# Routed rows of a mixture of experts: 31 blocks of 256 and 9 of 128 in place of 39 of 256, with three buffers of weights

## The chip, the cores and the metric

The kernel runs as one program on one core of a Trainium2 chip. The metric is the device time of one execution in microseconds (us). TensorE (PE in the profile; its weight loads are listed apart as PEld), VectorE (DVE), ScalarE (ACT), GpSimd (POOL) and SyncE (SP) each work through their own list of instructions in order. They wait for one another only through semaphores, and DMA transfers are issued from these lists too, here mostly from SP, ACT and POOL. The TensorE clock that the chip grants varies; the profile shows it as a share of full speed.

## The reference

Two transformer layers on x of shape (4, 1024, 256), that is 4,096 rows of D = 256, all in float32. Each layer is an attention and a feed-forward part, each on the layer-normalised x and added to it. The change is in the first layer's feed-forward, a mixture of eight routed and two shared experts (H = 512 hidden values, K = 2 experts per row):

```python
def _swiglu_stacked(x, w1, b1, w2, b2, w3, b3):
    p1 = jnp.einsum('btd,ndh->nbth', x, w1) + b1[:, None, None, :]
    p2 = jnp.einsum('btd,ndh->nbth', x, w2) + b2[:, None, None, :]
    glu = jax.nn.silu(p1) * p2
    return jnp.einsum('nbth,nhd->nbtd', glu, w3) + b3[:, None, None, :]
...
scores = jax.nn.softmax(x @ gate_w + gate_b, axis=-1)
weights, indices = jax.lax.top_k(scores, K)
routed_all = _swiglu_stacked(x, rw1, rb1, rw2, rb2, rw3, rb3)
...
routed = jnp.sum(weights[..., None] * gathered, axis=2)
shared = _swiglu_stacked(x, sw1, sb1, sw2, sb2, sw3, sb3).mean(axis=0)
return shared + routed
```

The reference computes all eight experts for all rows and picks two; a kernel has to compute only the two that were chosen, which is 8,192 rows of expert work in all. How many rows each expert gets is known only at run time.

## The kernel before

The whole kernel is one function, `two_layers`. It keeps x in SBUF as 32 tiles of 128 rows. A scheduler orders the instructions of each engine from the program's order, their dependencies and the number of buffers of each tile; nothing is ordered by hand in this part. The first feed-forward (from L508) runs in these steps.

1. The eight units of 512 rows are normalised and transposed (`xnT_f0`), and the gate's logits are computed (`gate`, L567). Meanwhile SP loads the first shared expert's weights and fills the scratch array `xs_d` in device memory with zeros (L689).
2. `shared(e, weights, u)` (L634) is the feed-forward of a shared expert on unit u: 16 up-matmuls of 512 columns (L643), an activation on ACT (L651) and a product on DVE (L652) for each of the four blocks f of 128 hidden values, then 16 down-matmuls of 256 columns (L660). The units of the first shared expert are spread over the time in which the routing is computed.
3. `choose` (L589) marks the two experts of each row on DVE. Running sums by matmul (L720, L725) give each row its place among the rows of its expert (`pos`). DVE then finds how many blocks of BT = 256 rows each expert needs (`over`, `blocks`), where each expert begins (`ends`, `begins`), the slot of each row (`slot`), the expert that owns each block (`owner`), and each block's biases (`b_blk`).
4. POOL scatters the rows to their slots in `xs_d` with 64 indirect DMAs (L799). Under them TensorE goes on with shared units.
5. The routed blocks (L817): NBLK = 39 blocks of 256 rows, enough for every split of the 8,192 rows over eight experts. For block n, SP reads the owner from SBUF into a register (L818), loads that expert's weights w1, w2 and w3, 512 KB each (`load_expert`, L625; pool `epool`, two buffers), the bias b3 spread over all partitions (L823), and the block's rows `xb` (L827, two buffers). TensorE transposes the rows (L833), ACT copies them (`xbT`, L839), and the up-matmuls take 128x128 pieces of w1 and w2 as stationary and xbT, 256 columns, as moving operand (L847). Two f share one tile of two PSUM banks. ACT and DVE make `glu_b` of it (L857, L860). The down-matmuls take glu_b as stationary and w3 as moving operand (L871), DVE adds b3 (`yb`, L879), and ACT issues the write to `ys_d` (L885).
6. The second shared expert's other six units (L890), and under them POOL gathers each row's two results from `ys_d` (L898) and DVE adds them, weighted, to x (L904).

The scheduler places the transposes of the next block between the down-matmuls of a block, where TensorE would wait for the products.

Of the kernel before, what the change touches and what calls it, by code (L numbers as in the profile page):

```python
# [8 lines left out]
F32 = mybir.dt.float32  # L9
F32R = mybir.dt.float32r  # L10
BF16 = mybir.dt.bfloat16
I32 = mybir.dt.int32
U32 = mybir.dt.uint32
AF = mybir.ActivationFunctionType
ALU = mybir.AluOpType
AX = mybir.AxisListType
PSUM = bass.MemoryType.PSUM

P = 128
D = 256  # L20
NB = 4
S = 1024
NT = NB * S // P
# [6 lines left out]
E = 8  # L30
FF = 512
NF = FF // P
# [7 lines left out]
def two_layers(  # L40
# [33 lines left out]
    nc = tc.nc  # L74
# [28 lines left out]
    for i in range(NT):  # L103
# [15 lines left out]
        out=dsel,  # L119
        in_=dsel,  # L120
# [384 lines left out]

    with ExitStack() as lc:  # L508
        wpool = lc.enter_context(tc.tile_pool(name="f0_w", bufs=1))
        epool = lc.enter_context(tc.tile_pool(name="f0_e", bufs=2))  # L510
        pool = lc.enter_context(tc.tile_pool(name="f0", bufs=2))
        xnT = wpool.tile([P, 2, NT * P], F32, name="xnT_f0")
        dram = lc.enter_context(tc.tile_pool(name="f0_d", bufs=1, space=bass.MemoryType.DRAM))
        NE = E + 2
        BT = 2 * P
        NBLK = NT * P * 2 // BT + E - 1
        NSHARE = NT * P // BT

        xs_d = dram.tile([NBLK * BT, D], F32, name="xs_d")
        ys_d = dram.tile([NBLK * BT, D], F32, name="ys_d")  # L520
        gw = wpool.tile([P, 2, E], F32, name="gw")
        nc.sync.dma_start(out=gw, in_=gate0_w.rearrange("(k p) e -> p k e", p=P))
        gb = wpool.tile([P, E], F32, name="gb")
# [21 lines left out]
        )  # L545
        ones_b = wpool.tile([P, P], BF16, name="ones_b")
        nc.gpsimd.memset(ones_b, 1.0)
        full_i = wpool.tile([P, NSHARE], I32, name="full_i")
        nc.gpsimd.iota(full_i, pattern=[[BT, NSHARE]], base=0, channel_multiplier=0)
        full = wpool.tile([P, 1, NSHARE], F32, name="full")  # L550
        nc.vector.tensor_copy(full[:, 0, :], full_i)
        blk_i = wpool.tile([P, NBLK], I32, name="blk_i")
        nc.gpsimd.iota(blk_i, pattern=[[1, NBLK]], base=0, channel_multiplier=0)
        blk = wpool.tile([P, NBLK, 1], F32, name="blk")
        nc.vector.tensor_copy(blk[:, :, 0], blk_i)

# [32 lines left out]
        def choose():  # L589


            def t2(name):
                return small.tile([P, NT, 1], F32, tag=f"{name}_g", name=name)

            def wide(a):
                return a.to_broadcast([P, NT, E])

            v = nc.vector
            m = t2("m")
            v.tensor_reduce(m[:, :, 0], logits, AX.X, ALU.max)  # L600
            v.tensor_tensor(logits, logits, wide(m), ALU.subtract)
            pr = wpool.tile([P, NT, E], F32, name="pr")
            nc.scalar.activation(pr, logits, AF.Exp)
            sm = t2("sm")
            v.tensor_reduce(sm[:, :, 0], pr, AX.X, ALU.add)
            v.reciprocal(sm, sm)
            v.tensor_tensor(pr, pr, wide(sm), ALU.mult)

            for k in range(2):
                v.tensor_reduce(weight[k][:, :, 0], pr, AX.X, ALU.max)  # L610
                eq = wpool.tile([P, NT, E], F32, name=f"eq{k}")
                v.tensor_tensor(eq, pr, wide(weight[k]), ALU.is_equal)
                v.tensor_tensor(eq, eq, down.to_broadcast([P, NT, E]), ALU.mult)
                ck = t2("ck")
                v.tensor_reduce(ck[:, :, 0], eq, AX.X, ALU.max)
                v.tensor_tensor(picked[k], eq, wide(ck), ALU.is_equal)
                if k == 0:
                    v.scalar_tensor_tensor(pr, picked[0], -2.0, pr, ALU.mult, ALU.add)
            v.tensor_tensor(marks, picked[0], picked[1], ALU.add)
# [64 lines left out]
        first = load_expert(sw1[0], sw2[0], sw3[0])  # L684
        zeros = wpool.tile([P, 1, D], F32, name="zeros")
        nc.gpsimd.memset(zeros, 0.0)
        xs_fill = xs_d[:, :].rearrange("(p n r) d -> n p r d", p=P, r=13)
        for n in range(NBLK * 2 // 13):
            nc.sync.dma_start(out=xs_fill[n], in_=zeros.to_broadcast([P, 13, D]))  # L689


        roots(0, NT)
# [31 lines left out]
        for i in range(NT):  # L724
# [9 lines left out]
        nc.vector.tensor_copy(pos, pos_ps)  # L734

        v = nc.vector
        over = wpool.tile([P, E, NSHARE], F32, name="over")
        v.tensor_tensor(
            over,
            pos[:, NT, :].unsqueeze(2).to_broadcast([P, E, NSHARE]),  # L740
            full.to_broadcast([P, E, NSHARE]),
            ALU.is_gt,
        )
        blocks = wpool.tile([P, E], F32, name="blocks")
        v.tensor_reduce(blocks, over, AX.X, ALU.add)
        ends = blocks
        for step in (1, 2, 4):
            sums = wpool.tile([P, E], F32, name=f"ends{step}")
            v.tensor_copy(sums[:, :step], ends[:, :step])
            v.tensor_tensor(sums[:, step:], ends[:, step:], ends[:, :-step], ALU.add)  # L750
            ends = sums
        begins = wpool.tile([P, 1, E], F32, name="begins")
        v.tensor_tensor(begins[:, 0, :], ends, blocks, ALU.subtract)
        v.tensor_scalar(begins, begins, float(BT), None, ALU.mult)
        v.tensor_tensor(
            pos[:, :NT, :], pos[:, :NT, :], begins.to_broadcast([P, NT, E]), ALU.add
        )
        slots = []
        for k in range(2):
            v.tensor_tensor(picked[k], picked[k], pos[:, :NT, :], ALU.mult)  # L760
# [3 lines left out]
            v.tensor_copy(slot, slot_f)  # L764
            slots.append(slot)

        past = wpool.tile([P, NBLK, E], F32, name="past")
        v.tensor_tensor(
            past,
            ends.unsqueeze(1).to_broadcast([P, NBLK, E]),  # L770
            blk.to_broadcast([P, NBLK, E]),
            ALU.is_le,
        )
        owner = wpool.tile([P, NBLK, 1], F32, name="owner")
        v.tensor_reduce(owner[:, :, 0], past, AX.X, ALU.add)
        v.tensor_scalar(owner, owner, E - 1.0, None, ALU.min)
        owner_i = wpool.tile([P, NBLK], I32, name="owner_i")
        v.tensor_copy(owner_i, owner[:, :, 0])
        v.tensor_tensor(
# [34 lines left out]
            shared(E + 1, second, u)  # L814


        for n in range(NBLK):  # L817
            e = nc.sync.value_load(owner_i[0:1, n : n + 1], min_val=0, max_val=E - 1)  # L818
            w1_t, w2_t, w3_t = load_expert(
                *(w[bass.ds(e, 1)].rearrange("e k f -> (e k) f") for w in (rw1, rw2, rw3))  # L820
# [4 lines left out]
            )  # L825
            xb = pool.tile([P, 2, D], F32, tag="xb", name="xb", bufs=2)
            nc.sync.dma_start(  # L827
                out=xb, in_=xs_d[n * BT : (n + 1) * BT, :].rearrange("(a p) d -> p a d", p=P)
            )
            ps = one_bank()  # L830
            for kc in range(2):
                for a in range(2):
                    nc.tensor.transpose(  # L833
                        ps[:, (2 * kc + a) * P : (2 * kc + a + 1) * P],
                        xb[:, a, kc * P : (kc + 1) * P],
                        ident,
                    )
            xbT = pool.tile([P, 2, BT], F32, tag="xbT", name="xbT")
            nc.scalar.copy(xbT.rearrange("p k t -> p (k t)"), ps)  # L839
            glu = pool.tile([P, NF, BT], F32, tag="glu", name="glu_b")  # L840
            for fp in range(NF // 2):
                ps = two_banks()
                for m, w_t in enumerate((w1_t, w2_t)):
                    for ff in range(2):
                        f = 2 * fp + ff
                        for kc in range(2):
                            mm(  # L847
                                ps[:, (2 * m + ff) * BT : (2 * m + ff + 1) * BT],
                                lhsT=w_t[:, kc, f * P : (f + 1) * P],
                                rhs=xbT[:, kc, :],  # L850
                                start=(kc == 0),
                                stop=(kc == 1),
                            )
                for ff in range(2):
                    f = 2 * fp + ff
                    act = pool.tile([P, BT], F32, tag="act", name="act_b", bufs=3)
                    nc.scalar.activation(  # L857
                        act, ps[:, ff * BT : (ff + 1) * BT], AF.Silu, bias=b_blk[0][:, f, n : n + 1]
                    )
                    nc.vector.scalar_tensor_tensor(  # L860
                        glu[:, f, :],
                        ps[:, (2 + ff) * BT : (3 + ff) * BT],
                        b_blk[1][:, f, n : n + 1],
                        act,
                        ALU.add,
                        ALU.mult,
                    )
            ps = one_bank()
            for a in range(2):
                for f in range(NF):  # L870
                    mm(  # L871
                        ps[:, a * D : (a + 1) * D],
                        lhsT=glu[:, f, a * P : (a + 1) * P],
                        rhs=w3_t[:, f, :],
                        start=(f == 0),
                        stop=(f == NF - 1),
                    )
            yb = pool.tile([P, 2, D], F32, tag="yb", name="yb")
            nc.vector.tensor_tensor(  # L879
                yb,  # L880
                ps.rearrange("p (a d) -> p a d", a=2),
                b3_t.to_broadcast([P, 2, D]),
                ALU.add,
            )
            nc.scalar.dma_start(  # L885
                out=ys_d[n * BT : (n + 1) * BT, :].rearrange("(a p) d -> p a d", p=P), in_=yb
            )


# [848 lines left out]
```

## Time and profile before

| | |
|---|---|
| median of 3 runs | 2569.44 us (2560.59 to 2582.25) |
| the profiled execution | 2580.51 us, span 2578.6 us |
| mean granted TensorE clock | 0.941 |
| busy over the span | PE 2328.3 us (90%), PEld 1389.6 (54%), DVE 1396.7 (54%), ACT 986.0 (38%), POOL 640.4 (25%) |
| up-matmuls of the routed blocks, L847 | 1,248 records, 275.8 us busy, from 729.0 us on |
| down-matmuls, L871 | 624 records, 161.8 us busy |
| transposes, L833 | 156 records, 29.6 us busy |
| weights of routed experts | 117 transfers of 512 KB |

How to read it: times are counted from the first instruction. One f32 matmul of the program appears as two records on PE, each with a weight load on PEld, so 16 up-matmuls are 32 records. A record's own duration contains the latency through the array, and successive records overlap; how fast they follow each other is read from their starts. In rows of the timeline the columns are start, duration, engine, line, operation, tiles and count, and in brackets the engine's idle time before the row and what ended it.

### The profile page before, as it was taken

The numbers are of one execution on the slowest core, as the hardware profiler recorded it, in microseconds if no ns is written. First come the engines' busy times: TensorE is split into PE (matmuls) and PEld (weight loads), VectorE is DVE, ScalarE is ACT, GpSimd is POOL, SyncE is SP. The second block draws the span as 40 slices with busy tenths as digits, with TensorE's granted clock in tenths as the row PEclk, the third lists the DMA queues.
The fourth block names the chain that finished last, engine by engine and source line by source line (L and its number), as shares of the span: only waits on it lengthen the run. The fifth ranks groups of instructions, "written<-read, shape, count | busy, mean of one in ns | idle before, by whom it ended". The sixth has DMA issues, their size and how long they took to land.

```text
span 2578.6 us, 42321 instructions
## 1 busy us (share of the span) xinstructions
PE 2328.3 (90%) x16882; PEld 1389.6 (54%) x16882; DVE 1396.7 (54%) x2272; ACT 986.0 (38%) x1345; POOL 640.4 (25%) x741
## 2 busy tenths in 40 slices
PE   6999999899999999999957999999999999997534
PEld 3566666566578888885533444444444444443322
DVE  6445445514222222224536777676767798994293
ACT  1333333221122222221112666565656565665311
POOL 2333333601700000004340013122221211124354
PEclk8998999899999999999976999999999999998667
DMA  3000000510266666663143231312131312100134
GB/s 92 17 10 10 10 13 8 166 48 23 104 185 196 194 192 194 194 192 88 51 98 68 52 74 52 67 43 68 43 68 43 67 43 67 43 19 11 54 118 131
DMA packets 202976, 207.52 MB, mean 80 GB/s; under 512 B 89128, under 2 KB 163496, under 8 KB 202780
## 3 DMA queue, kind: packets, MB, share of 16 engines
q1 hardware_dynamic: 179292, 163.37, 23.4%
q0 software_dynamic: 11792, 30.18, 3.9%
q10 hardware_dynamic: 11696, 11.27, 1.3%
q8 instruction: 133, 2.18, 0.4%
q14 instruction: 63, 0.52, 0.1%
HBM read 141.49 MB, written 58.80 MB: 78 GB/s over the span
## 4 chain that ended last, share of the span: by engine, by line
PE 72%; DVE 15%; ACT 4%; issue 4%; DMA 2%; POOL 2%; SPq 0%; POOLq 0%; ACTq 0%; DVEq 0%
PE two L847 10%; PE two L1416 10%; PE acc L1431 8%; PE two L643 7%; DVE tops L1381 6%; PE two L329 5%; PE two L1374 4%; PE acc L871 4%; PE two L258 2%; PE two L1296 2%; PE misc L660 2%; PE acc L660 2%; PE two L321 2%; PE acc L396 1%; DVE glu_b L860 1%
## 5 line engine op out<-in xcount | busy, mean ns | idle before, releaser
L1381 DVE TENSOR_REDUCE tops<-two 128x2 f32<-128x1024 f32 x512 | 619.0, 1217 | 126.7 <-PE two L1374 124.7
L1424 ACT ACTIVATE pT<-two 128x1024 f32<-128x1024 f32 x512 | 523.5, 1025 | 329.1 <-PE two L1416 324.5
L1431 PE MATMUL acc<-pT,v_t 128*32 128x256 f32 x4096 | 345.0, 397 | 5.4 <-ACT pT L1424 5.4
L1416 PE MATMUL two<-q_st,k_st 64*128 64x512 f32 x1024 | 261.2, 503 | 32.2 <-DVE tops L1381 19.7
L847 PE MATMUL two<-xbT,w_t 128*128 128x256 f32 x1248 | 275.8, 379 | 0.7 <-ACT xbT L839 0.7
L847 PEld LDWEIGHTS two<-xbT,w_t 128*128 128x128 f32 x1248 | 237.0, 190 | 33.1 <-ACT xbT L839 0.9
L1374 PE MATMUL two<-k_st,q_st 64*128 64x512 f32 x1024 | 232.1, 421 | 20.1 <-DMA k_st<-halves 9.3
L643 PE MATMUL two<-xnT_f,w_t 128*128 128x512 f32 x512 | 229.8, 601 | 3.1 <-DVE glu L652 3.1
L1416 PEld LDWEIGHTS two<-q_st,k_st 64*128 64x128 f32 x1024 | 97.2, 185 | 225.0 <-issue 127.9
L860 DVE SCALAR_TENSOR_TENSOR glu_b<-two,b_blk,act_b 128x256 f32<-128x256 f32 x156 | 75.3, 483 | 249.4 <-ACT act_b L857 249.4
L1416 PE MATMUL two<-top_st,minus 64*128 64x512 f32 x1024 | 208.2, 401 | 0.0
L857 ACT ACTIVATE act_b<-two,b_blk 128x256 f32<-128x256 f32 x156 | 74.0, 474 | 330.6 <-PE two L847 287.6
L898 POOL DMA_INDIRECT yr<-ys_d,slot x64 | 61.4, 960 | 538.1 <-DMA ys_d<-yb 471.1
L1431 PEld LDWEIGHTS acc<-pT,v_t 128*32 128x32 f32 x4096 | 86.8, 108 | 167.9 <-issue 145.8
L871 PE MATMUL acc<-w_t,glu_b 128*128 128x256 f32 x624 | 161.8, 392 | 6.4
L1374 PEld LDWEIGHTS two<-k_st,q_st 64*128 64x128 f32 x1024 | 107.6, 191 | 92.4 <-DVE tops L1381 28.9
L643 PEld LDWEIGHTS two<-xnT_f,w_t 128*128 128x128 f32 x512 | 96.3, 192 | 111.7 <-issue 105.7
L355 DVE TENSOR_REDUCE top<-two 128x4 f32<-128x768 f32 (+1 forms) x128 | 112.5, 919 | 71.3 <-PE two L329 71.3
L381 POOL TENSOR_SCALAR_AFFINE_SELECT pT<-pT 128x1024 f32<-128x1024 f32 x64 | 70.4, 1100 | 305.5 <-ACT pT L378 305.5
L378 ACT ACTIVATE pT<-two 128x768 f32<-128x768 f32 (+1 forms) x128 | 93.7, 783 | 121.2 <-PE two L329 120.7
L651 ACT ACTIVATE act<-two,bT 128x512 f32<-128x512 f32 x64 | 44.0, 687 | 241.8 <-PE two L643 230.7
L871 PEld LDWEIGHTS acc<-w_t,glu_b 128*128 128x128 f32 x624 | 112.2, 189 | 37.5 <-DVE glu_b L860 25.2
(304 smaller groups left out, 3110.9 us busy)
## 6 DMA issues: line engine op xcount, KB each, us to landing
w_t<-in_L_ffn_rw_dram SPq DMA_DIRECT2D x117, 512.0 KB
halves<-split SPq DMA_DIRECT2D x64, 256.0 KB
q_st<-halves SPq DMA_DIRECT2D x128, 128.0 KB
k_st<-halves SPq DMA_DIRECT2D x256, 64.0 KB
xs_d<-zeros SPq DMA_DIRECT2D x6, 1664.0 KB
xb<-xs_d SPq DMA_DIRECT2D x39, 256.0 KB
ys_d<-yb ACTq DMA_DIRECT2D x39, 256.0 KB
b_t<-in_L_ffn_rb_dram SPq DMA_DIRECT2D x39, 128.0 KB
```

What stands on the lines that cost most here:

```text
L329: mm(parts[r][:, gg, :], lhsT=left[32 * r : 32 * r + rows, g, l0 : l0 + P], rhs=right[32 * r : 32 * r + rows, g, r0 : r0 + n], start=(mask ...
L355: nc.vector.tensor_reduce(tops[i][:, 2 * ab : 2 * ab + 2, 2 * gp : 2 * gp + 2], scs[ab], AX.X, ALU.max)
L643: mm(ps[:, n * 512 : (n + 1) * 512], lhsT=w_t[:, kc, f * P : (f + 1) * P], rhs=xnT[:, kc, cols], start=(kc == 0), stop=(kc == 1),)
L660: mm(ps[:, jj * D : (jj + 1) * D], lhsT=glu[:, f, j * P : (j + 1) * P], rhs=w3_t[:, f, :], start=(f == 0), stop=(f == NF - 1),)
L847: mm(ps[:, (2 * m + ff) * BT : (2 * m + ff + 1) * BT], lhsT=w_t[:, kc, f * P : (f + 1) * P], rhs=xbT[:, kc, :], start=(kc == 0), stop=(kc ...
L860: nc.vector.scalar_tensor_tensor(glu[:, f, :], ps[:, (2 + ff) * BT : (3 + ff) * BT], b_blk[1][:, f, n : n + 1], act, ALU.add, ALU.mult,)
L871: mm(ps[:, a * D : (a + 1) * D], lhsT=glu[:, f, a * P : (a + 1) * P], rhs=w3_t[:, f, :], start=(f == 0), stop=(f == NF - 1),)
L1374: mm(sc[:, hh], lhsT=q_st[rows, j * P : (j + 1) * P], rhs=k_st[rows, kk * 512 : (kk + 1) * 512], start=True, stop=True,)
L1381: newest["vector"] = nc.vector.tensor_reduce(tops[:, :, j, kk], sc, AX.X, ALU.max).ins
L1416: mm(sc[:, hh * 512 : (hh + 1) * 512], lhsT=minus[rows] if top else k_st[rows, k * P : (k + 1) * P], rhs=(top_ring[p % 2] if top else q_st ...
L1424: newest["scalar"] = nc.scalar.activation(pt, sc, AF.Exp).ins
L1431: newest["tensor"] = mm(oT_ps[32 * r : 32 * r + 32, hh * D : (hh + 1) * D], lhsT=vals[n // HU][:, n % HU, k, :], rhs=pts[r // 2][:, hh * 5 ...
```

## The change

The slots are laid out in tiles of 128 rows instead of blocks of 256. An expert whose number of tiles is odd has a last tile alone. NTILE = 71 tiles cover every split. They are cut into PAIRS = 31 blocks of two tiles, which come first in `xs_d`, and nine blocks of one tile behind them, 40 blocks in all. If the run-time pairs are fewer than 31, the singles are moved up to begin behind the 31st (`gap`). `order` fixes at build time in which order the blocks are computed: a single follows after three or four pairs, and the last block is a single.

A block of one tile has up-matmuls of 128 columns, with all four f in one tile of two PSUM banks (`fs = 4`), half as many down-matmuls and transposes, and half the rows to read and write. Its weights and its b3 are loaded as for a block of two.

The index work on DVE changes with it: `over` compares with 32 instead of 16 thresholds, even and odd tiles are counted apart, running sums go over 16 instead of eight entries, each row gets one of two offsets (`behind`), and the owner is found among 16 ends. `epool` has three buffers of weights instead of two. `eq0`, `eq1`, `over` and `behind` share one buffer.

```diff
-        epool = lc.enter_context(tc.tile_pool(name="f0_e", bufs=2))
+        epool = lc.enter_context(tc.tile_pool(name="f0_e", bufs=3))
...
-        NBLK = NT * P * 2 // BT + E - 1
+        NTILE = 2 * NT + E - 1
+        PAIRS = (NTILE - E - 1) // 2
+        NBLK = NTILE - PAIRS
+        order = []
+        for n in range(PAIRS):
+            order.append((2 * n, 2, n))
+            if (n + 1) * (NBLK - PAIRS) // PAIRS > n * (NBLK - PAIRS) // PAIRS:
+                n = PAIRS + n * (NBLK - PAIRS) // PAIRS
+                order.append((PAIRS + n, 1, n))
...
-        blocks = wpool.tile([P, E], F32, name="blocks")
-        v.tensor_reduce(blocks, over, AX.X, ALU.add)
-        ends = blocks
-        for step in (1, 2, 4):
+        tiles = wpool.tile([P, 2, E], F32, name="tiles")
+        v.tensor_reduce(
+            tiles, over.rearrange("p e (t o) -> p o e t", o=2), AX.X, ALU.add
+        )
+        v.tensor_tensor(tiles[:, 0, :], tiles[:, 0, :], tiles[:, 1, :], ALU.subtract)
...
+        for step in (1, 2, 4, 8):
...
+        v.tensor_tensor(behind, pos[:, :NT, :], paired.to_broadcast([P, NT, E]), ALU.is_ge)
+        v.tensor_tensor(behind, behind, begins[:, 1:, :].to_broadcast([P, NT, E]), ALU.mult)
...
+        v.tensor_tensor(pos[:, :NT, :], pos[:, :NT, :], behind, ALU.add)
...
-        for n in range(NBLK):
+        for t0, nt, n in order:
+            cols = nt * P
+            rows = slice(t0 * P, t0 * P + cols)
...
-            for fp in range(NF // 2):
+            fs = 512 // cols
+            for f0 in range(0, NF, fs):
                 ps = two_banks()
                 for m, w_t in enumerate((w1_t, w2_t)):
-                    for ff in range(2):
-                        f = 2 * fp + ff
+                    for ff in range(fs):
+                        f = f0 + ff
                         for kc in range(2):
                             mm(
-                                ps[:, (2 * m + ff) * BT : (2 * m + ff + 1) * BT],
+                                ps[:, m * 512 + ff * cols : m * 512 + (ff + 1) * cols],
                                 lhsT=w_t[:, kc, f * P : (f + 1) * P],
-                                rhs=xbT[:, kc, :],
+                                rhs=xbT[:, kc, :cols],
...
-            for a in range(2):
+            for a in range(nt):
                 for f in range(NF):
...
-                out=ys_d[n * BT : (n + 1) * BT, :].rearrange("(a p) d -> p a d", p=P), in_=yb
+                out=ys_d[rows, :].rearrange("(a p) d -> p a d", p=P), in_=yb[:, :nt]
```

The zero fill covers 71 rows of `xs_d` per partition in six transfers of 12 or 11 rows, instead of 78 in six of 13.

## The prediction

> **What bounds the kernel now.** I read the page's busy row and its 40 slices first, then the stretches of 50 us, then one block instruction by instruction.
>
> ```profile
> PE   6999999899999999999957999999999999997534
> ...
> PEclk8998999899999999999976999999999999998667
> ...
> GB/s 92 17 10 10 10 13 8 166 48 23 104 185 196 194 192 194 194 192 88 51 98 68 52 74 52 67 43 68 43 68 43 67 43 67 43 19 11 54 118 131
> ```
>
> Slices 11 to 17 (from 709 us on) are the routed blocks: TensorE at 9, its clock at 9, the transfers at a steady 194 GB/s. The stretches of this stage, whose columns are busy us of PE, PEld, DVE, ACT and POOL, then granted clock, DMA share and GB/s:
>
> ```profile
> 850.00:900.00 50.00, 49.15 (x227) 41.00 (x226) 11.46 (x22) 11.47 (x23) 0.00 (x0) 1.00 0.68 194
> 900.00:950.00 50.00, 49.33 (x229) 41.58 (x228) 11.17 (x21) 9.93 (x20) 0.00 (x0) 1.00 0.65 190
> ```
>
> PE 99% busy, DVE and ACT under 25%, DMA two thirds. So the stage's length is its TensorE work, and its unit is one block:
>
> ```profile
> 901.37 6.88 PEld L847 LDWEIGHTS two<-xbT,w_t 128*128 128x128 f32 x32
> ...
> 908.27 0.84 PEld L871 LDWEIGHTS acc<-w_t,glu_b 128*128 128x128 f32 x4
> ...
> 908.75 0.47 ACT L857 ACTIVATE act_b<-two,b_blk 128x256 f32<-128x256 f32 x1 [1.96 <-PE two L847]
> 909.14 0.35 PEld L833 LDWEIGHTS misc<-ident,xb 128*128 128x128 f32 x2
> 909.26 0.48 DVE L860 SCALAR_TENSOR_TENSOR glu_b<-two,b_blk,act_b 128x256 f32<-128x256 f32 x1 [1.95 <-ACT act_b L857]
> ...
> 909.79 0.30 PEld L871 LDWEIGHTS acc<-w_t,glu_b 128*128 128x128 f32 x2 [0.30 <-DVE glu_b L860]
> ...
> 910.82 2.02 PEld L871 LDWEIGHTS acc<-w_t,glu_b 128*128 128x128 f32 x10 [0.34 <-DVE glu_b L860]
> ...
> 912.87 6.88 PEld L847 LDWEIGHTS two<-xbT,w_t 128*128 128x128 f32 x32
> ```
>
> Period: 912.87 - 901.37 = **11.50 us**; 39 blocks, 448.5 us. An f32 matmul is two records, each with a load. Up: 32 records in 6.88 us, 0.215 each for 256 columns. Down: 16 records of 0.215, 3.44. Four transposes of the next block, 0.5. Waits for the chain activation, product, activation, product: 0.30 + 0.34.
>
> **What goes: 39 pairs become 31.** Eight pairs, 8 x 11.50 = 92.0 us, all on TensorE and so on the path.
>
> **What comes: nine singles of 128 rows.** TensorE has 16 up matmuls of 128 columns instead of 256 (32 records), 4 down (8 records, still 256 wide: 8 x 0.215 = 1.72) and 2 transposes (2 x 0.107 = 0.21). The trace of before has no full-array f32 matmul of 128 columns with a load in front. The stream alone is half of 0.215, 0.107. The load's own pace shows where the matmul is tiny:
>
> ```profile
> 600.88 1.40 PE L572 MATMUL misc<-gw,xnT_f 128*128 128x8 f32 x12
> 602.14 1.10 PE L643 MATMUL two<-xnT_f,w_t 128*128 128x512 f32 x2
> ...
> 621.70 0.27 PE L720 MATMUL acc<-marks,before_m 128*128 128x256 bf16 x1
> 621.80 2.05 PE L725 MATMUL acc<-marks,ones_b 128*128 128x256 bf16 x32
> 623.71 13.98 PE L643 MATMUL two<-xnT_f,w_t 128*128 128x512 f32 x32
> ...
> 1340.46 1.97 PE L1336 MATMUL misc<-wv_t,xnT_a 128*64 128x128 f32 x32
> ```
>
> The gate: 12 f32 records of 8 columns in 602.14 - 600.88 = 1.26 us, 0.105 each, which is the load. So a single's record is 0.107 if load and stream overlap, 0.212 if they alternate. Two rows say overlap. L1336 loads 64 columns and streams 128 on half the array, 32 records in 1.97 less the last one's 0.27: 0.055 each, so per 0.109 us two loads of 64 columns each and 128 streamed columns on either half. L720 and L725 stream 4,480 columns in all in 2.01 us; at 0.215 us per 512 that alone is 1.88, so 33 loads of 128 columns cost 4 ns each over it. I take **0.109**: 32 x 0.109 = 3.49.
>
> The rule that speaks against it: the Trainium skill (TensorE: Matmul & The Clock Gate, "Back-to-back issue gap") says that in a stream of load and matmul both set the spacing, 81 ns sustained at 128 columns against 56 without loads. That ratio, 1.46, gives 0.159 per record, 1.6 us more a single and 14.4 us in all. I take the rows, which are of this kernel, and keep the rule for the range.
>
> Waits of a single, by the program's order of after (the code is there, unrun) and these durations: activation 0.37 for 128 columns (0.474 for 256 and 0.687 for 512, by a line), product 0.35 (0.483 and 0.745), copy of 256 columns 0.37 (L165), of 512 columns 0.59.
> - Before it: its copy xbT stands on ACT behind the pair's last activation, and TensorE's first two matmuls of the single stand before the pair's last down-matmuls. Copy done about 2.4 us after the pair's last up-load; the pair's tail then ends at 5.05 us with 0.94 idle, where it had 0.64: +0.3.
> - In it: all four f lie in one tile, so no activation starts before all 32 records end. TensorE has the next block's four transposes (0.45), then waits for the first product: 0.38 + 0.37 + 0.35 + 0.07 for hand-overs, 1.2 - 0.45 = 0.7. On ACT the next pair's xbT copy stands between the single's first and second activation, so that pair's up starts 0.9 us after the transposes; the other three products are covered by the next pair's first up-matmuls, which the order puts between them, but for some 0.1.
>
> Single: 3.49 + 1.72 + 0.21 + 0.3 + 0.8 = **6.5 us**; bounds 5.4 (waits hidden) and 9.8 (loads alternate). Nine: 58.5. Stage: 31 x 11.50 + 58.5 = 415.0, **33.5 us less**.
>
> **Third weight buffer and transfers.** A pair moves 1.5 MiB of weights, 0.125 of bias, 0.25 in, 0.25 out: 2.23 MB, in 11.50 us 194 GB/s, as measured. A single still needs all weights: 1.97 MB in 6.5 us, 302 GB/s; at share 0.67 for 194 the engines would hold 290. So one single can't feed itself, but the mean is 86.8 MB in 415 us, 209 GB/s, share 0.72. SP's order of after issues weights n behind the bias of n-1, which waits for yb of n-3: two blocks ahead, at worst 18.0 - 1.4 = 16.6 us, where 1.97 MB at 290 need 6.8. The xb of n+1 stands behind w3 of n, which waits for the down of n-3, long done. Cost 0; without that cover each single would wait.
>
> **Index work on DVE before the scatter.** 17 more DVE instructions. Pace: small dependent ones 0.18, 128x256 ones 0.42, `ended` (640 wide) 0.8 twice. Slots come about 5 us later than 628.75. Behind them on POOL stand the 64 scatters (1.27 each), so the first xb is issued near 717 instead of 711.8; it lands in some 3 us and TensorE wants it at 727.7: hidden, 8 us spare. Shared products of the same unit are queued behind it: the fourth (639.05 to 639.8) ends near 641.2, and TensorE, which reaches that down-matmul at 639.25 in the order of after, waits for it. Before it waited 0.15: **+1.7 us**. SP's value loads (629 to 653) now have block 0's weights amid them; the xb wait hides it. The zero fill writes 71/78 of before, ended at 512.6 long before the scatter: 0. `eq` and `over` sharing a buffer run in turn anyway: 0.
>
> **Hand-over behind the last block.** TensorE already waits there, since products stand behind gathered rows on DVE:
>
> ```profile
> 1195.51 4.11 PE L660 MATMUL misc<-w_t,glu 128*128 128x256 f32 x10 [3.16 <-DVE glu L652]
> ```
>
> After: the last block is a single and its ys write comes four shared records (1.7 us) later, but two gathered rows fewer (2.5 us) stand before the fourth product. I take 0, bounds -3 and +3.
>
> **Sum.** -33.5 + 1.7 = -31.8. The profiled execution: 2580.5 us (span 2578.6) becomes 2548.7. It lies 11 us above the median of three runs, 2569.4; from that, **2537.6**.
>
> **Rivals.**
> - *Loads bare under short matmuls.* Same page, "The mechanism": a load overlaps running matmuls only in other row groups (elsewhere the page also names a background buffer). By that a record is 0.105 + 0.107, the single 9.8, the stage 444.7, total 2567. Against: 0.215 at 256 columns has no room for 0.105, and the two rows above. Paced by the 81 ns rule: single 8.1, 2552.
> - *Slower: the whole load latency in front of each matmul.* A load record lasts 0.190; followed by 0.107 of stream it is 0.297, the single 12.5, nine 112.5, the stage 469.0: +20.5 + 1.7 gives 2592. It decides at a single of 10.0 us, 0.218 a record. [...]Against: the gate's 0.105 is under 0.190, so latency isn't in the pace.
> - *Transfers bound.* If 194 GB/s were the ceiling, a single takes 1.97 MB / 194 = 10.1 us, the stage 447.4, total 2570. Against: share 0.67, and SP's waits for released buffers.
> - *It doesn't do what it says:* singles computed 256 wide would give 40 x 11.5 = 460, 2583. The order lists 16 matmuls of 128x128 for each, so I give it nothing.
>
> **Chances.** Forecast 0.76; 81 ns pace 0.09; no gain (bare loads or transfers) 0.10; slower 0.05. 1% is 25.7 us, about what a measurement of this kernel can tell from no change (three runs spread over 21.7). The forecast clears it by 6, so 0.69 of its 0.76 counts as faster; of the pace case 0.03; no gain gives 0.08 same and 0.02 slower; the slow one 0.01 and 0.04. Faster 0.72, same 0.22, slower 0.06. Range: waits hidden, 2528, less 10 for scatter, to the pace case, 2552, plus 9: 2518 to 2561.
>
> **What the profile after would show.** A pair's period stays 11.50; a single's up-records take 3.5 us; from a pair's first up-load to the next pair's across a single are 18.0 us; clock 1.00 and 205 to 212 GB/s in the stage; about 0.7 us of TensorE wait for the product in each single. Wrong if: up-records at 0.16 or more; TensorE waiting for w_t or xb; the clock below 1.00 there; the saving in the stage given back after 1,150 us.

## The result, and the profile after

The changed kernel takes **2543.55 us** (median of four runs, 2538.59 to 2548.45) where the kernel before took 2569.61 (2560.59 to 2582.25, four runs): ratio 0.9875, 95% interval 0.985 to 0.990. The forecast was 2537.6. The profiled execution is the run of 2548.45 us, span 2546.3; the forecast for the profiled execution was 2548.7.

The page of the changed kernel, its slices in tenths and its GB/s (the routed blocks are slices 11 to 17, as before):

```profile
PE   6999999799999999998948999999999999997534
...
PEclk8988999899999999999968999999999999998667
...
GB/s 93 18 10 10 11 12 10 125 77 3 131 160 212 205 206 230 206 172 75 50 118 68 35 68 44 68 44 68 44 68 43 68 44 67 44 19 11 54 120 132
```

The stage is still TensorE at 9 with its clock at 9, but the transfers are at 205 to 230 GB/s in slices 12 to 16 instead of 194. The next line is the first of the stretches of 50 us that were shown of before (busy us of PE, PEld, DVE, ACT and POOL, then granted clock, DMA share, GB/s). The second, 900 to 950 us, has PE at 48.90, a DMA share of 0.65 and 215 GB/s:

```profile
850.00:900.00 50.00, 48.89 (x241) 41.42 (x240) 12.34 (x25) 11.54 (x25) 0.00 (x0) 1.00 0.64 214
```

PE is 98% busy instead of 99%: the singles bring a wait that pairs don't have. One single in the timeline of the weight loads (start, duration, engine, line, operation, tiles, count, idle time before and what ended it). L893 are up-loads, L876 transposes, L920 down-loads:

```profile
805.62 6.88 PEld L893 LDWEIGHTS two<-xbT,w_t 128*128 128x128 f32 x32
812.53 0.84 PEld L920 LDWEIGHTS acc<-w_t,glu_b 128*128 128x128 f32 x4
...
814.82 0.52 PEld L893 LDWEIGHTS two<-xbT,w_t 128*128 128x128 f32 x4 [0.47 <-ACT xbT L882]
815.26 2.03 PEld L920 LDWEIGHTS acc<-w_t,glu_b 128*128 128x128 f32 x10
817.31 3.31 PEld L893 LDWEIGHTS two<-xbT,w_t 128*128 128x128 f32 x28
820.54 0.47 PEld L876 LDWEIGHTS misc<-ident,xb 128*128 128x128 f32 x4
821.72 0.30 PEld L920 LDWEIGHTS acc<-w_t,glu_b 128*128 128x128 f32 x2 [0.70 <-DVE glu_b L909]
...
834.84 6.88 PEld L893 LDWEIGHTS two<-xbT,w_t 128*128 128x128 f32 x32
...
846.34 6.88 PEld L893 LDWEIGHTS two<-xbT,w_t 128*128 128x128 f32 x32
```

The single's 32 up-records are the four from 814.82 to 815.26 and the 28 from 817.31 to 820.54: 0.44 + 3.23 = 3.67 us, 0.110 and 0.115 a record. These two are means that hold the edges of their groups: taken one by one, the starts of the weight loads are 0.111 to 0.112 us apart, except for the first steps of each group (0.216 in the group of 28, which is still the last down-matmul's). From 820.54 to 821.72 come the next pair's four transposes and 0.70 us of waiting for the single's first product. Between the starts of pairs' up-loads, a pair is 11.50 us as before (846.34 - 834.84). From 805.62 to 834.84 it is 29.22 us: two pairs, the second of which has its first up-loads among the single's down-loads, and a single of 6.22 us between them. The first single takes 6.48 us, seven take 6.21 to 6.22, and the last one, whose waits the shared expert's matmuls fill, 6.06.

Where the time went, by the starts of TensorE's weight loads at the same marks in both profiled executions:

| stretch | before | after | difference |
|---|---|---|---|
| start to the first xb transposes | 727.5 | 728.8 | +1.3 |
| from there to the second shared expert's first down-matmul behind the blocks ("the stage" in what follows) | 462.56 | 426.59 | **-36.0** |
| from there to layer 1's first transposes | 136.7 | 135.4 | -1.3 |
| layer 1 to the end | 1251.8 | 1255.5 | +3.7 |
| span | 2578.6 | 2546.3 | -32.3 |

Only the second row and 0.5 us of the first (the index work, told below) belong to the change, as the experiments show: the stage repeats from one profiled run to another within 0.1 us, and the rest doesn't.

### The profile page after: what moved, and what is told of

Same layout as the page of the kernel before. It is cut to its first block, busy times and chain, and to the rows that moved or that the text cites. A ratio compares the mean times of both kernels' runs of the same rounds, so it can differ in the third digit from the quotient of the medians.

```text
span 2546.3 us, 42216 instructions
## 1 busy us (share of the span) xinstructions
PE 2291.9 (90%) x16844; PEld 1361.5 (53%) x16844; DVE 1398.2 (55%) x2294; ACT 980.1 (38%) x1350; POOL 639.7 (25%) x742
## 5 line engine op out<-in xcount | busy, mean ns | idle before, releaser
L1465 PE MATMUL two<-q_st,k_st 64*128 64x512 f32 x1024 | 262.0, 504 | 31.8 <-DVE tops L1430 19.5
L893 PE MATMUL two<-xbT,w_t 128*128 128x256 f32 (+1 forms) x1280 | 257.9, 356 | 1.3 <-ACT xbT L882 0.7
L893 PEld LDWEIGHTS two<-xbT,w_t 128*128 128x128 f32 x1280 | 222.7, 190 | 31.1 <-ACT xbT L882 5.1
L909 DVE SCALAR_TENSOR_TENSOR glu_b<-two,b_blk,act_b 128x256 f32<-128x256 f32 (+1 forms) x160 | 72.6, 454 | 228.7 <-ACT act_b L903 228.7
L903 ACT ACTIVATE act_b<-two,b_blk 128x256 f32<-128x256 f32 (+1 forms) x160 | 71.9, 450 | 310.9 <-PE two L893 159.5
L657 PEld LDWEIGHTS two<-xnT_f,w_t 128*128 128x128 f32 x512 | 96.4, 193 | 114.1 <-issue 105.8
L920 PE MATMUL acc<-w_t,glu_b 128*128 128x256 f32 x568 | 148.5, 390 | 8.3 <-DVE glu_b L909 4.0
L1525 POOL TENSOR_TENSOR y<-y,rows_b 128x256 f32<-128x256 f32 x32 | 23.4, 733 | 431.6 <-DVE y L1522 431.6
```

Of the source, the lines that this page charges most:

```text
L657: mm(ps[:, n * 512 : (n + 1) * 512], lhsT=w_t[:, kc, f * P : (f + 1) * P], rhs=xnT[:, kc, cols], start=(kc == 0), stop=(kc == 1),)
L893: mm(ps[:, m * 512 + ff * cols : m * 512 + (ff + 1) * cols], lhsT=w_t[:, kc, f * P : (f + 1) * P], rhs=xbT[:, kc, :cols], start=(kc == 0), ...
L903: nc.scalar.activation(act[:, :cols], ps[:, ff * cols : (ff + 1) * cols], AF.Silu, bias=b_blk[0][:, f, n : n + 1],)
L909: nc.vector.scalar_tensor_tensor(glu[:, f, :cols], ps[:, 512 + ff * cols : 512 + (ff + 1) * cols], b_blk[1][:, f, n : n + 1], act[:, :cols ...
L920: mm(ps[:, a * D : (a + 1) * D], lhsT=glu[:, f, a * P : (a + 1) * P], rhs=w3_t[:, f, :], start=(f == 0), stop=(f == NF - 1),)
L1465: mm(sc[:, hh * 512 : (hh + 1) * 512], lhsT=minus[rows] if top else k_st[rows, k * P : (k + 1) * P], rhs=(top_ring[p % 2] if top else q_st ...
```

## The experiments

Three theories stood against each other. **TensorE**: the stage is as long as TensorE's own records and its waits for products, and transfers and the third buffer are off the path. **Transfers**: part of the gain is the third buffer's, or the singles' loads hold the stage up. **Loads**: a short matmul does not cover its weight load. The experiments ran in two sessions. In the first of them, which has the first eight kernels and ran on another chip (0) than the second (11), everything, the kernel before too, took some 70 us more (median of before 2641.5 to 2642.6, and 2573.2 in the second); where that lies is told at the end. Ratios are to the kernel before in the same session; the stage is compared across sessions.

### The third buffer

```diff
-        epool = lc.enter_context(tc.tile_pool(name="f0_e", bufs=3))
+        epool = lc.enter_context(tc.tile_pool(name="f0_e", bufs=2))
```

> The changed kernel with two buffers of weights instead of three. Theory (TensorE's own work sets the stage, the third buffer buys nothing): w1 and w2 of a block can be issued when the up-matmuls two blocks before have ended, so even across a single they have 4.8 + 6.2 = 11.0 us, and w3 as long; 1.97 MB need 6.8 us at 290 GB/s. Stage (first xb transposes to the second shared expert's first down-matmul) stays 426.8 us within 1, period of a pair 11.50, across a single 17.7, total as the changed kernel (ratio to before 0.985 to 0.99). Rival (part of the gain is the third buffer): TensorE waits for w_t in or behind each single, 1 us or more each, the stage 10 us or more longer, ratio 0.991 or above.

Measured: stage 426.68 us, ratio 0.988 (0.983 to 0.994). TensorE's waits in the stage (who waited for what, us in total, times, longest) hold no weight tile and no xb. The largest are for products, and with three buffers they are 23.5 us in 64 times:

```profile
PEld acc L920 <- DVE glu_b L909: 23.6, 64, 1.0
PEld two L657 <- issue: 6.0, 25, 0.2
PEld two L893 <- ACT xbT L882: 5.2, 10, 0.9
```

The other way round, the kernel before with three buffers (`eq0` and `eq1` share one buffer to make room):

```diff
-        epool = lc.enter_context(tc.tile_pool(name="f0_e", bufs=2))
+        epool = lc.enter_context(tc.tile_pool(name="f0_e", bufs=3))
```

> The kernel before with three buffers of weights (eq0 and eq1 share a buffer to make room). Theory: 0, the stage from the first xb transposes to the second shared expert's first down-matmul stays 462.8 us within 1, ratio 0.997 to 1.003. Rival (third buffer is part of the gain): 5 us or more faster, ratio below 0.998, stage 458 or less.

Measured: stage 462.59 us, ratio 1.001 (0.999 to 1.003). The third buffer is worth nothing in either kernel. The gain is the blocks'.

### The singles' transfers

The singles take the weights of the pair before them and load none of their own (so they are computed with the wrong expert):

```diff
-            w1_t, w2_t, w3_t = load_expert(
-                *(w[bass.ds(e, 1)].rearrange("e k f -> (e k) f") for w in (rw1, rw2, rw3))
-            )
+            if nt == 2:
+                w1_t, w2_t, w3_t = load_expert(
+                    *(w[bass.ds(e, 1)].rearrange("e k f -> (e k) f") for w in (rw1, rw2, rw3))
+                )
```

> The changed kernel with the nine singles using the weights of the pair before them: their w1, w2, w3 (13.5 MiB) are not loaded, so singles are computed with the wrong expert. Theory (transfers hidden): nothing, the stage 426.8 us within 1, ratio 0.985 to 0.99. Rival (the singles' loads hold the stage up): each single without its 6.8 us of transfer is faster, the stage 5 us or more shorter.

Measured: stage 426.63 us, ratio 0.988 (0.983 to 0.993). From 850 to 950 us the transfers fall from 214 and 215 GB/s to 178 and 173, and TensorE is as busy as before to a hundredth of a us:

```profile
850.00:900.00 50.00, 48.89 (x242) 41.43 (x241) 12.06 (x25) 11.07 (x24) 0.00 (x0) 1.00 0.53 178
```

The loads of 13.5 MiB are hidden entirely. How much room is left was tried by crowding the singles:

```diff
-        order = []
-        for n in range(PAIRS):
-            order.append((2 * n, 2, n))
-            if ...
+        order = [(2 * n, 2, n) for n in range(PAIRS)]
+        order += [(PAIRS + n, 1, n) for n in range(PAIRS, NBLK)]
```

> The changed kernel with the nine singles behind all 31 pairs, not spread among them. Nine singles in a row want 1.97 MB each per some 5.7 us, 345 GB/s. Theory: the engines carry at most 290 to 330 GB/s (0.65 of the time busy at 194 to 215), so behind the two blocks of lead a single takes 6.0 to 6.8 us, and TensorE shows waits for w_t for the first time; the stage comes out 426.8 us, between -3 and +5. Rival (194 GB/s is the ceiling): 10.1 us a single, the stage 25 to 35 us longer. Rival (no ceiling in sight): singles next to each other run at 5.6, the stage 3 to 5 us shorter, no wait for w_t.

Measured: stage 427.43 us, 0.8 more, ratio 0.989 (0.985 to 0.992). It lies within the theory's bounds, but its mechanism wasn't there: TensorE waits for no w_t. Next to each other singles take 6.35 us, and what each waits for is the copy of its rows:

```profile
1149.77 0.30 PEld L889 LDWEIGHTS two<-xbT,w_t 128*128 128x128 f32 x2 [0.80 <-ACT xbT L878]
...
1156.11 0.30 PEld L889 LDWEIGHTS two<-xbT,w_t 128*128 128x128 f32 x2 [0.80 <-ACT xbT L878]
```

The copy needs the transposes, and they stand behind the up-matmuls of the single before. All 71 tiles as blocks of one tile:

```diff
+        order = [(t, 1, t // 2) for t in range(2 * PAIRS)]
+        order += [(PAIRS + n, 1, n) for n in range(PAIRS, NBLK)]
...
-            e = nc.sync.value_load(owner_i[0:1, n : n + 1], min_val=0, max_val=E - 1)
+            if t0 % 2 == 0 or n >= PAIRS:
+                e = nc.sync.value_load(owner_i[0:1, n : n + 1], min_val=0, max_val=E - 1)
```

> The changed kernel with all 71 tiles as blocks of one tile (each loads its own weights, 71 x 1.97 MB). TensorE work of one: 32 up-records at 0.114 = 3.66, 8 down-records 1.72, 2 transposes 0.21: 5.6 us, which would want 352 GB/s. Theory: transfers bind here, at 290 to 330 GB/s, so 6.0 to 6.8 us a block, 71 blocks 426 to 483 us, TensorE waits for w_t and xb, DMA share 0.95 or more. Rival (194 GB/s is the ceiling): 10.1 us a block, 717 us. Rival (TensorE still binds): 5.6 to 5.8 a block, 398 to 412 us, no wait for w_t.

Measured: stage 464.06 us, ratio 1.002 (1.000 to 1.004); again 6.35 us a block, with the same 0.80 for xbT and no wait for w_t. One stretch of it:

```profile
1000.00:1050.00 50.00, 45.49 (x334) 42.00 (x333) 14.28 (x39) 13.54 (x40) 0.00 (x0) 1.00 0.94 310
```

The transfers deliver 310 GB/s where the kernel before draws 194, so 194 was a demand and not a ceiling. A share of 0.94 suggests that little is left, but it is no measure of it: in this stage the share has not followed the GB/s. The same with two buffers:

```diff
-        epool = lc.enter_context(tc.tile_pool(name="f0_e", bufs=3))
+        epool = lc.enter_context(tc.tile_pool(name="f0_e", bufs=2))
```

> All 71 tiles as blocks of one tile, with two buffers of weights. With three the period was 6.35 us at 309 to 314 GB/s, a DMA share of 0.89 to 0.94, and no wait for w_t. Theory (this is where the third buffer counts): a buffer is free for the next load 2.7 us (w1, w2) before the end of its block or 3.4 us (w3) into the next one, which leaves about 9 us from issue to need, and the transfers, which have to carry 1.97 MB in every 6.35 us, have next to nothing to spare: waits for w_t appear, period 6.5 to 7.5, stage 475 to 540. Rival (9 us are enough): 464 within 1, no wait for w_t.

Measured: stage 473.22 us, 9.2 more than with three, just under the theory's 475; ratio 1.005 (1.003 to 1.007). Most blocks still take 6.35 us, but waits that three buffers didn't have appear. In the same view of waits as above, now with PE's own rows:

```profile
PE two L890 <- DMA w_t<-in_L_ffn_rw_dram: 6.6, 6, 2.3
PE two L890 <- ACT act_b L900: 6.5, 3, 2.7
```

So of the orders tried, the third buffer counts only in the one where every block is a single. (By the starts of their up-loads, most blocks take 6.35 us and ten take more, 9.1 us more in all. That each of these waited for weights is inferred from the two rows, not shown wait by wait.)

### The single itself

The nine singles left out of `order` (their rows are not computed, and their part of `ys_d` is filled with zeros in one transfer):

```diff
-        order = []
-        for n in range(PAIRS):
-            order.append((2 * n, 2, n))
-            if ...
+        order = [(2 * n, 2, n) for n in range(PAIRS)]
```

> The changed kernel without its nine singles (their rows are not computed; their part of ys is zeros, written in one transfer during the zero fill). Theory: a single inside the stage takes 6.22 us of TensorE (first one 6.49), the last one 6.06: 56.0 us less than the changed kernel, total near 2488, stage 370.8. By the forecast's 6.5 each: 58.5 less, stage 368.3. If singles cost only what TensorE's busy time in them is (5.6 us each), 50 less.

Measured: stage 370.68 us, 55.9 less; ratio 0.967 (0.962 to 0.972). That is 6.21 a single, where the forecast had 6.5. Then, for the record's pace, only 64 columns of a single in its up-matmuls, activations and products (GpSimd sets the other half of its `glu_b` to zero):

```diff
+            cut = cols if nt == 2 else 64
...
-                                rhs=xbT[:, kc, :cols],
+                                rhs=xbT[:, kc, :cut],
```

> The changed kernel with only 64 of a single's 128 rows in its up-matmuls, activations and products (the other half of its glu is zeros, set by GpSimd). Load and stream overlap by my theory, so a record takes the longer of load (0.105) and stream (0.107 at 128 columns, 0.054 at 64): the record stays at 0.105 to 0.110, 32 of them 3.4 to 3.5 instead of 3.66, and with shorter activations the single is 0.2 to 0.5 us shorter, 2 to 5 us in all. Rival (load and stream alternate in part, or the stream alone sets the pace): the record falls to 0.055 to 0.08, the up-records to 1.8 to 2.6 us, the single 1.1 to 1.9 us shorter, 10 to 17 us in all.

Measured: stage 425.46 us, 1.1 less in all, 0.13 a single, a little under the theory's 2 to 5; ratio 0.988 (0.985 to 0.991). A single's up-loads there:

```profile
890.56 3.09 PEld L896 LDWEIGHTS two<-xbT,w_t 128*128 128x128 f32 x26
893.51 0.48 PEld L876 LDWEIGHTS misc<-ident,xb 128*128 128x128 f32 x4
```

26 records in 893.51 - 890.56 = 2.95 us, 0.1135 each, where 128 columns have 0.115. Half the stream costs the same. Taken one by one, the starts are 0.111 to 0.112 us apart at 64 columns and at 128, and so are those of the gate's matmuls of 8 columns (L572 of the kernel before). So the load sets the pace up to 128 columns, and the stream of 128, 0.107 as half of 0.215, just fits beside it; nothing alternates.

### A faster version

A pair's 11.50 us hold 0.64 us of waits for products. The next block's transposes and copy are put in front of the down-matmuls, these run f by f over both tiles, and a single's up-matmuls use two PSUM tiles:

```diff
+        coming = ready(*order[0])
+        for at, (t0, nt, n) in enumerate(order):
+            w1_t, w2_t, w3_t, b3_t, xbT = coming
...
-            fs = 512 // cols
+            fs = 2
...
+            if at + 1 < len(order):
+                coming = ready(*order[at + 1])
             ps = one_bank()
-            for a in range(nt):
-                for f in range(NF):
+            for f in range(NF):
+                for a in range(nt):
...
-                        start=(f == 0),
+                        start=(f == 0 and a == 0),
```

(`ready` holds the block's loads, transposes and copy, unchanged. How much each of the three edits brings was not tried.)

> A version meant to be faster: each block's transposes and its xbT copy are put in front of the down-matmuls of the block before, down-matmuls run f by f over both tiles (both in one PSUM bank), and a single's up-matmuls take two PSUM tiles of two f. Theory (what is left beside TensorE's own work in a pair's 11.50 us are the 0.64 us of waits for products): the down-matmuls of f 0 and 1 and the four transposes, 2.2 us, cover the products of f 2 and 3 (ready 1.6 and 2.6 us behind the last up-load), a pair's period becomes 6.90 + 0.50 + 3.44 = 10.84, 31 pairs 20 us less; singles 0 to 0.3 us less each; stage 404 to 407 us, total near 2522, ratio 0.981, demand 221 GB/s still met. Rival (the waits were cover for transfers or for the copy): the period stays above 11.2 with waits for xbT or w_t instead, stage 418 or more.

Measured: stage 398.99 us, 27.6 less than the changed kernel; ratio 0.977 (0.973 to 0.982). A pair's period in its weight loads, without a wait:

```profile
879.12 6.88 PEld L900 LDWEIGHTS two<-xbT,w_t 128*128 128x128 f32 x32
886.02 0.57 PEld L876 LDWEIGHTS acc<-ident,xb 128*128 128x128 f32 x4
886.57 3.32 PEld L929 LDWEIGHTS misc<-w_t,glu_b 128*128 128x128 f32 x16
889.91 6.88 PEld L900 LDWEIGHTS two<-xbT,w_t 128*128 128x128 f32 x32
```

889.91 - 879.12 = 10.79, and a single is 5.53 (two pairs and a single from 852.00 to 879.12, 27.12 us). That is what their records alone add up to: for a single 32 of 0.112, 8 of 0.216 and 2 transposes of 0.109 make 5.53. The stage came out under the expected 404 to 407 us, mainly because the singles gained 0.69 us each and not 0 to 0.3. With two buffers of weights:

> next_rows_first with two buffers of weights instead of three. TensorE is 100% busy there and the transfers carry 219 to 250 GB/s. Theory: the lead is still 9 us or more against some 6.3 us for 1.97 MB at 310 GB/s, so stage 399.0 within 1. Rival (with the waits gone the third buffer starts to matter): waits for w_t around the singles, stage 402 or more.

Measured: stage 398.99 us, the same to the hundredth, so the third buffer isn't missed here either. This is the fastest version: **2508.79 us** in its session, ratio 0.975 (0.970 to 0.980). The kernel before in this order:

```diff
-            for a in range(2):
-                for f in range(NF):
+            for f in range(NF):
+                for a in range(2):
```

> The kernel before with next_rows_first's order in its 39 pairs (two buffers, no singles). Theory: a pair's period falls from 11.50 to 10.80 here too, 39 x 0.70 = 27.3 us, stage 462.6 - 27.3 = 435.3 within 1, ratio 0.988 to 0.992; so the change's own gain stays 36.3 us (435.3 - 399.0) whether TensorE's waits are there or not. Rival (the order pays only with three buffers or with singles): stage above 440.

Measured: stage 435.41 us, ratio 0.988 (0.982 to 0.994). The order takes 27.2 us from the kernel before and 27.6 from the changed one, and the change takes 435.41 - 398.99 = 36.4 us with the order and 36.0 without it. The two gains add.

### The rest of the span

> The changed kernel itself, in the same session as the experiments, where the kernel before took some 2642 us and not 2569 and ACT stood still for 60 to 83 us under the scatter in every profile of it. Theory (what differs between sessions lies outside the routed blocks): stage 426.6 within 0.5, ratio to before 0.985 to 0.99, ACT's stand under the scatter seen again with this very kernel if it belongs to the session; from layer 1's first transposes to the end 1251 to 1257 us, as in all runs so far. Rival (the 3.7 us that layer 1 took longer in the changed kernel's first profile belong to the change): 1255 us or more again, while the kernel before stays near 1252.

Measured: 2538.49 us (2536.68 to 2548.03), ratio 0.986 (0.981 to 0.991), stage 426.59. The medians of the second session differ by 34.7 us, nearly the stage's 36.0, where those of the first result differ by 26.1. The first result's are of four executions each, which spread over 22 us before and 10 us after. Layer 1 to the end took 1254.1 us in its profile. With the blocks of before it took 1251.8, 1255.8 (before_three_buffers) and 1254.2 (before_next_rows_first), and over all the profiles 1251.8 to 1257.2 whichever kernel ran: the 3.7 us of the table are the spread of single executions. So are the 1.3 us behind the stage, where the same stretch runs from 133.6 to 138.1 us.

## Why the prediction was right, point by point

- **Bound, and pairs at 11.50 us.** Right: pairs at 11.50, clock 1.00, and 212 GB/s from 764 to 1,082 us (slices 12 to 16) against 205 to 212 forecast.
- **Record of 0.109.** Right in kind, since load and stream overlap, but 5% short over the 32 records: 3.67 us instead of 3.49. The load's pace was read too low. The gate's 12 records in 1.26 us give 0.105 only because the first step is 0.03; the other eleven are 0.111 to 0.112, as in the singles. That is about half of the 0.18 us, and the edges of the two groups are the rest. The rows L720 and L725 were no support for the f32 record: at 0.105 a load, their 32 bf16 loads would need 3.4 us, and the rows took 2.01, so those loads are quicker than f32's. L1336, which is f32, does support it. By the Trainium skill (TensorE: Matmul & The Clock Gate, "Back-to-back issue gap"), 81 ns against 56, the estimate was 0.159. By its "The mechanism", a load that overlaps only matmuls of other row groups, it was 0.212 (the page also names a background weight buffer, which no run here shows or rules out). The measurement decides against both for these matmuls. What half_columns adds is which of the two sets the pace: the load.
- **Waits around a single, +0.3 before it and 0.8 in it.** The first did not come. The tail of the pair, forecast at 5.05 us with 0.94 idle, took 4.78 (812.53 to 817.31) with 0.30 + 0.47 idle. A pair's tail is 4.60; two transposes fewer (0.21) and four of the single's records (0.44) make 4.83 of it, so nothing is lost there. The second came as 0.70 in the row, and 6.22 - 3.67 - 1.72 - 0.21 + 0.05 = 0.67 in the sum.
- **Single of 6.5, nine 58.5, stage -33.5.** Measured 6.22, 56.0 and -36.0. Three terms were off: the records cost 0.18 more, the wait before 0.35 less (-0.05 for +0.3), the waits inside 0.13 less. The mis-sized wait before a single is the largest of them.
- **Third buffer and transfers 0.** Right, by four kernels. The estimate of 290 GB/s was too low, for 310 were carried. The DMA share did not rise to the forecast 0.72: from 764 to 1,082 us it is 0.65 at 212 GB/s, and in the kernel before, from 764 to 1,146 us, 0.67 at 194. A ceiling worked out from the share was therefore unsound.
- **Index work +1.7.** Mis-sized: +0.5. From the first running-sum matmul (bf16, 256 columns) to the first xb transposes it is 105.8 us in the kernel before and 106.3 in the changed one, 105.9 and 106.3 in the second session's pair of kernels with the other order. The slots came 5.2 us later (633.96 for 628.75), as forecast, and xb was issued at 716.7, as forecast. But the fourth product, forecast to end near 641.2, started at 639.92 and took 0.74, so the loads of the down-matmuls waited 0.91 where they had waited 0.40 (after, then before):

```profile
640.71 2.02 PEld L674 LDWEIGHTS misc<-w_t,glu 128*128 128x128 f32 x10 [0.91 <-DVE glu L666]
639.85 2.02 PEld L660 LDWEIGHTS misc<-w_t,glu 128*128 128x128 f32 x10 [0.40 <-DVE glu L652]
```

- **Hand-over 0.** Measured -1.3, not to be told from the spread.
- **Total.** -31.8 forecast and -32.3 measured between the profiled executions. That they agree so closely is luck: -2.5 in the stage and -1.2 in the index work meet +3.7 of spread in layer 1. The median came 6 us above the forecast, since the forecast took the profiled run's 11 us above the median of before as standing for after too, where it was 5: that offset, too, is the spread of single executions.
- **Rivals.** Bare loads (0.212), load latency (0.297) and the 81-ns pace (0.159) fall with the record's pace of 0.112; "transfers bound at 194" falls with 310 in all_singles. The singles are computed 128 wide: 288 records of L893 on PE are of 128 columns.

## What to carry to other kernels

Before splitting blocks finer, find at which width the weight load overtakes the stream: here going from 256 to 128 columns nearly halves a record (0.215 to 0.112 us), and going on to 64 saves nothing (0.112). Don't take what the transfers draw for what they can carry: look for the ceiling with a crowded order before paying for a buffer. When TensorE is the bound, its waits inside a block are worth more than they look: 0.7 us in each of 40 blocks are 28 us, and reordering what is there anyway recovered them.

## What the runs showed of the hardware that was not expected

In the session of the first eight kernels ACT stood still under the scatter of 64 indirect DMAs, 80 to 83 us in all, in every profile, with "remote" or "issue" named as what ended it; TensorE ran dry behind it and its clock fell to 0.50. The same changed kernel in the other session shows none of it, nor do the first profiles. ACT's rows of the kernel with two buffers of weights:

```profile
648.72 0.69 ACT L665 ACTIVATE act<-two,bT 128x512 f32<-128x512 f32 x1 [26.81 <-remote]
670.42 0.69 ACT L665 ACTIVATE act<-two,bT 128x512 f32<-128x512 f32 x1 [21.02 <-issue]
```

In most of these profiles one activation comes in the time of 17 scatters (21.7 us at 1.27 each). From the running-sum matmul to the first xb transposes it makes 172.7 us out of 106.3, which is nearly all of what that session was slower by. It hits both kernels alike and ends before the routed blocks. Session and chip changed together, so the record can't tell which of the two it goes with, and its cause was not tried.
